# When the row sums leave PSUM, when they are used, and how the norm statistics are cut: three moves in a two-layer graph attention kernel

## The chip, the cores and the metric

The kernel runs on one core of a Trainium2 chip. The metric is the device time of one execution in microseconds (us). The core has a matrix engine (PE; its weight loads are listed apart as PEld), a vector engine (DVE), an activation engine (ACT), a general engine (POOL), and a queue engine (SP) that issues nearly all transfers. Each works through its own instructions in the order in which the program lists them; between engines there are semaphores.

## The reference, cut to what matters

There are 8 batch elements of 2048 nodes with 256 features, and one adjacency matrix for all. Layer 0 is masked attention with 4 heads of 64 features and a residual, with two layer norms behind it; layer 1 is a graph attention with two layer norms fewer:

```python
scores = clip(einsum(q, k) / 8, -10, 10);  scores = where(mask == 0, -10, scores)
attn = softmax(scores);  out = einsum(attn, v) @ Wo.T + bo + x
x = layernorm(x + layernorm(out) * gamma + beta)                      # end of layer 0
e = leaky_relu(s_i[:, None] + s_j[None, :]);  e = where(adj | eye, e, -inf)
x = layernorm(x + elu(softmax(e) @ Wh))                               # end of layer 1
```

A softmax in layer 0 runs over chunks of 256 keys, not over all 2048: every chunk has its own row sums, and the chunks' outputs are added after each is divided by its own sums.

## The kernel before, in words

**Layer 0.** An element has 4 blocks of 512 queries (`NIB`), and a block has 8 chunks of 256 keys (`NCH`). One chunk of one block is an iteration `J` (256 in all), and each has two halves of 128 keys. A half is called a beat here, after the counter `beat`; beats 0 to 511 are those of layer 0, 64 to an element. A beat has the scores of two pairs of heads (tile `sc`, L989, in the two buffers of a PSUM pool), their clipping and masking in place on DVE (L1004), and their exponentials on ACT (tile `e`, L1013). The products with v (tile `u`, L895, in two parts) and the row sums (tile `s`, L909: a product with ones) follow an iteration or more later. `s` and both `u` tiles come from one PSUM pool, `ps_m`, of two buffers. ACT copies them out: the sums to `ds` (L921), the products to `un` (L1055).

**From the sums to the division.** `inverses` (L917 to L948) copies the sums to `ds` and has SP send one row of each head to `dc` (L923), so that 128 partitions hold 16 values each. Then come, put on a list by beat (`at`): the reciprocal on DVE (L926), a store of it to DRAM (`rd`, L928), a load back that repeats each row for 32 partitions (`r`, L932), and `scaled`: the multiplication of `un` by `r` on DVE (L937 or L939) and, on POOL, its addition to `ctxT` (L940). What is on the list for a beat is emitted at the end of that beat.

**Layer 1 rides along.** When an element's layer 0 is done, its layer 1 runs inside the next element's beats: 64 steps of 128 keys by 512 queries. A step goes through ACT (`low` L723), DVE (`leaky` L727 and `edges` L732), ACT (`weights` L736), a POOL addition (`acc`, L747) and PE (`product`, L757, into the single PSUM buffer `us`). It is handed out at 1.5 steps per beat, so its 64 steps fill some 22 of the 32 iterations. Those are called open here, the others closed. In the code, `together` is true in an open iteration. There, half 0 has the sums of the iteration before the last (held back in the list `unsummed`, as POOL first has a transfer add the second half's exponentials to the first's, L1049) and both parts of `u`; half 1 has layer 1's products. In a closed iteration the sums and the first part of `u` are in half 0, the second part in half 1.

**Generators.** What stands behind a block is written as generators that advance one `yield` per beat. `fin` does layer 0's end of a block (projection `po`, two norms, transposes to `hT`), `fin1` that of layer 1 (tile `hx`, one norm, store to `out`, L620), `prelude` what layer 1 of an element needs first. `stats` (L310 to L322) has four pairs of bn_stats and bn_aggr on DVE (L315, L316), and one power on POOL (L321); `normalize` scales on ACT (L330). `short_pieces()` is true from beat 64 to beat 439. The tiles `x`, `y`, `hx` and `hr` have one buffer each.

What sets the order is the program text alone: nothing is reordered afterwards. The lines around the change:

Of the kernel before, what the change touches and what calls it, by code (L numbers as in the profile page):

```python
# [28 lines left out]
def tile_adj_attention__then__gat(  # L29
# [42 lines left out]
    NIB = N // IB  # L72
    TPB = IB // P
    NPAIR = H // 2
    NCH = N // CHUNK
# [234 lines left out]
    def stats(src, name):  # L310

        st = two.tile([P, TPB, 6], F32, tag="st", name=f"st_{name}")
        mv = two.tile([P, TPB, 2], F32, tag="mv", name=f"mv_{name}")
        for t in range(TPB):
            nc.vector.bn_stats(st[:, t, :], src[:, t, :])  # L315
            nc.vector.bn_aggr(mv[:, t, :], st[:, t, :])  # L316
            if t == TPB // 2 - 1 and beat < 2 * NIB * NCH:
                yield
        rstd = two.tile([P, TPB], F32, tag="rstd", name=f"rstd_{name}")
        nc.vector.tensor_scalar_add(rstd, mv[:, :, 1], EPS)  # L320
        nc.gpsimd.tensor_tensor(rstd, rstd, nhalf, ALU.pow)  # L321
        return mv, rstd  # L322
# [506 lines left out]
    def at(when, fn):  # L829
        agenda.setdefault(when, []).append(fn)  # L830
# [86 lines left out]
    def inverses(p, lag):  # L917


        ds = one.tile([P, IB], F32, tag="ds", name=f"ds{p['name']}")  # L920
        nc.scalar.copy(ds, p.pop("m"))  # L921
        p["dc"] = two.tile([P, IB // DH], F32, tag="dc", name=f"dc{p['name']}")
        nc.sync.dma_start(out=p["dc"], in_=ds.rearrange("(h m) (n w) -> h m n w", m=DH, n=DH)[:, 0, :, :])  # L923

        def inverse():
            nc.vector.reciprocal(p["dc"], p["dc"])  # L926
            p["rd"] = dram3.tile([H, IB], F32, tag="rd", name=f"rd{p['name']}")
            nc.sync.dma_start(out=p["rd"].rearrange("h (m w) -> (h m) w", m=DH), in_=p["dc"])  # L928

        def spread():  # L930
            p["r"] = two.tile([P, IB], F32, tag="r", name=f"r{p['name']}")
            nc.sync.dma_start(out=p["r"], in_=p["rd"].unsqueeze(1).to_broadcast([H, DH, IB]))  # L932

        def scaled():
            r2 = p["r"].unsqueeze(1).to_broadcast([P, 2, IB])
            if p["j"] == 0:
                nc.vector.tensor_mul(p["ctxT"], p["un"], r2)  # L937
            else:
                nc.vector.tensor_mul(p["un"], p["un"], r2)  # L939
                nc.gpsimd.tensor_add(p["ctxT"], p["ctxT"], p["un"])  # L940
            if p["j"] == NCH - 1:
                ctx_done[p["b"], p["ib"]] = beat
            if p["j"] == NCH - 3:
                fins.append(fin(p["b"], p["ib"], p["ctxT"]))

        at(beat + lag, inverse)
        at(beat + lag, spread)
        at(beat + 2 + 2 * lag, scaled)  # L948

    prev = None  # L950
    unsummed = []
# [1 line left out]
    for J in range(total + 1):  # L953
        b, ib, j = J // (NIB * NCH), J // NCH % NIB, J % NCH
        live = J < total
        if live and j == 0:
            ctxT = one.tile([P, 2, IB], F32, tag="ctx", name=f"ctxT{b}_{ib}")
        cur = {"b": b, "ib": ib, "j": j, "es": [], "ctxT": ctxT, "v": vs[min(b, B - 1)], "name": f"{b}_{ib}_{j}", "added": False}
        for half in range(2):
            c = 2 * j + half  # L960
            if live:

                if c % HT == 0:
                    if b == 0:
                        mk = blocks0[ib, c // HT]
                    else:
                        mk = mk0.pop((b, ib, c // HT))
                if c % HT == 1:
                    n = (b * NIB + ib) * 2 + c // HT + 1
                    nb, nib, nhf = n // (2 * NIB), n // 2 % NIB, n % 2  # L970
                    if 0 < nb < B:
                        mk0[nb, nib, nhf] = mask_block(0, nib, nhf, f"{nb}_{nib}_{nhf}")
            early = J < NIB * NCH
            rate = RATE if b < B - 1 else LAST_RATE
            if half == 0:
                together = prev is not None and live and l1_open()
            if not together:
                weights()
                waiting, flight["low"] = flight["low"], []
                take_lows(rate)  # L980
                new, flight["low"] = flight["low"], waiting
                leaky()
                flight["low"] = new
            scs = []
            if live:
                for hp in range(NPAIR):
                    sc = ps_s.tile([P, 2, IB], F32, tag="sc", name=f"sc{b}_{ib}_{c}_{hp}")
                    for h in range(2):
                        nc.tensor.matmul(  # L989
                            sc[:, h, :],  # L990
                            kTs[b][c // TPB][h * D : (h + 1) * D, hp, ts(c % TPB, P)],
                            qT[h * D : (h + 1) * D, hp, :],
                            start=True,
                            stop=True,
                        )
                    scs.append(sc)

            if half == 0:
                for p in unsummed:
                    sums(p)  # L1000
            if live:
                cap = mk[:, c % HT, :].unsqueeze(1).to_broadcast([P, 2, IB])
                for hp in range(NPAIR):
                    nc.vector.scalar_tensor_tensor(scs[hp], scs[hp], -CLIP, cap, ALU.max, ALU.min)  # L1004
                for hp in range(NPAIR):

                    e = one.tile(
                        [P, 2, IB],
                        F32,
                        tag=f"e{J % 2}_{(half + J // 2) % 2}_{hp}",  # L1010
                        name=f"e{b}_{ib}_{c}_{hp}",
                    )
                    nc.scalar.activation(e, scs[hp], AF.Exp)  # L1013
                    cur["es"].append(e)
                    if half == 0 and hp == 0:
                        for p in unsummed:
                            inverses(p, 0)
                        unsummed = []
            elif half == 0:
                for p in unsummed:  # L1020
                    inverses(p, 0)
                unsummed = []
            if not together:
                edges()
            elif half == 0:
                for s in flight["low"]:
                    s.leaky()
                    s.edges()
                flight["edged"] += flight["low"]
                flight["low"] = []  # L1030
            else:
                take_lows(2 * rate, 3.5)

            if prev is not None:
                if half == 0:
                    prev["un"] = three.tile([P, 2, IB], F32, tag="un", name=f"un{prev['name']}")
                    if not together:
                        sums(prev)
                        inverses(prev, 1 if early else 0)
                parts = (0, 1) if together and half == 0 else (half,) if not together else ()  # L1040
                ms = [ps_m.tile([P, IB], F32, tag="m", name=f"u{prev['name']}_{part}") for part in parts]
                for i in range(2):
                    for part, m in zip(parts, ms):
                        values(prev, part, m, i)
                    if together and half == 0 and i == 1:


                        for hp in range(NPAIR):
                            nc.gpsimd.dma_start(  # L1049
                                out=prev["es"][hp], in_=prev["es"][NPAIR + hp], accum_op=ALU.add  # L1050
                            )
                        prev["added"] = True
                        unsummed.append(prev)
                for part, m in zip(parts, ms):
                    nc.scalar.copy(prev["un"][:, part, :], m)  # L1055
            if together and half == 0:
                weights()

            end_beat(half == 1 or not together, half if together else None)
            if half == 1:  # L1060

                if live and j == NCH - 2 and J + 2 < total:
                    nb, nib = (b, ib + 1) if ib + 1 < NIB else (b + 1, 0)
                    xq = xT_tile(nb, nib, "q")
                if live and j == NCH - 1 and J + 1 < total:
                    qT = make_qT(nb, nib, xq)
            beat += 1
        prev = cur if live else None
# [55 lines left out]
```

## Time and profile before

| what | value |
|---|---|
| median of 3 runs | 4567.17 us (4559.63 to 4568.09) |
| the profiled execution's own time | 4558.66 us |
| its span, first to last instruction | 4556.9 us |
| busy: PE / DVE / ACT / POOL | 88% / 70% / 57% / 44% |
| granted clock of PE, mean | 0.957 |
| closed stretch of element 4, 2170 to 2320 us | PE 133.56 of 150.00 us busy, DVE 95.04, ACT 83.33 |
| open stretch of element 4, 2320 to 2710 us | PE 353.90 of 390.00 us busy, DVE 282.21, ACT 232.06 |
| after the last scores, 4269 to 4556 us | PE 191.73 of 287.00 us busy, DVE 222.25 |

The share of busy time is an average over stages with different limits, so each stage is read by itself. A wait in the profile is idle time of an engine just before an instruction, put down to what ended it. "PE u L895 <- ACT ds L921" reads: PE stood still ahead of a product of line 895 until ACT's copy of line 921 had been made. The two-buffer pool is why these are linked: the sums and the two parts of the product are three tiles.

### The profile page before, as it was taken

Reading aid. Unit: us, or ns where it says so; the run is one execution under the profiler, and the core shown is the slowest. Engines: PE = TensorE matmul, PEld = TensorE weight load, DVE = VectorE, ACT = ScalarE, POOL = GpSimd, SP = SyncE. Lnnn points to the kernel's source line nnn. Section 1 sums busy time; section 2 is a strip of 40 time slices with the busy share of each in tenths; the row PEclk is TensorE's granted clock in tenths of the full one; section 3 lists DMA queues with packets and bytes.
Section 4 is the critical chain, followed back from the end, with each engine's and each line's share of the span. In section 5 each row is a group of like instructions: output and inputs, shape, how many; then the busy total and the mean of one; then the engine's idle time right before and its main releaser. Section 6 shows DMA issues by size and latency. Waiting matters only on the chain. (4 is left out here: it accounts for less than half of the span.)

```text
span 4556.9 us, 59597 instructions
## 1 busy us (share of the span) xinstructions
PE 4004.2 (88%) x21845; PEld 1906.2 (42%) x21845; DVE 3188.2 (70%) x4530; ACT 2579.6 (57%) x3842; POOL 1989.5 (44%) x1203
## 2 busy tenths in 40 slices
PE   9889988899898888898899998899889899888767
PEld 3223334443344433444344543444334444344446
DVE  5886578755887557866588665876668756796777
ACT  5555555555566555655466555566555555565446
POOL 0232336553365434654346442555426545364520
PEclk9999999999999999999999999999999999999889
DMA  5554245543555435654356533655436554465521
GB/s 164 179 166 141 66 127 134 134 116 99 139 141 138 101 104 140 159 125 96 105 137 167 124 85 117 147 145 128 100 111 139 144 131 112 128 138 124 155 77 56
DMA packets 301125, 573.87 MB, mean 126 GB/s; under 512 B 90272, under 2 KB 125344, under 8 KB 299936
## 3 DMA queue, kind: packets, MB, share of 16 engines
q1 hardware_dynamic: 257344, 411.71, 30.3%
q0 software_dynamic: 43488, 158.35, 18.1%
q8 instruction: 171, 2.80, 0.3%
q14 instruction: 122, 1.00, 0.1%
HBM read 340.66 MB, written 68.88 MB: 90 GB/s over the span
## 5 line engine op out<-in xcount | busy, mean ns | idle before, releaser
L1013 ACT ACTIVATE e<-sc 128x1024 f32<-128x1024 f32 x1024 | 1045.6, 1026 | 1154.5 <-DVE sc L1004 1122.0
L1004 DVE SCALAR_TENSOR_TENSOR sc<-sc,mk 128x1024 f32<-128x1024 f32 x1024 | 1207.2, 1223 | 599.8 <-PE sc L989 498.7
L989 PE MATMUL sc<-qT,kT 64*128 64x512 f32 x4096 | 1079.1, 643 | 153.1 <-ACT e L1013 145.5
L895 PE MATMUL u<-e,v 128*32 128x512 f32 x8192 | 1011.9, 614 | 162.1 <-ACT ds L921 162.1
L757 PE MATMUL us<-wh,w 128*128 128x256 f32 x3584 | 854.7, 394 | 101.1 <-ACT w L736 53.3
L940 POOL TENSOR_TENSOR ctxT<-ctxT,un 128x1024 f32<-128x1024 f32 x224 | 569.0, 2540 | 696.6 <-DVE un L939 615.7
L757 PEld LDWEIGHTS us<-wh,w 128*128 128x128 f32 x3584 | 685.1, 195 | 322.3 <-ACT w L736 149.6
L747 POOL TENSOR_TENSOR acc<-acc,w 128x512 f32<-128x512 f32 x392 | 605.2, 1544 | 155.5 <-ACT w L736 136.0
L989 PEld LDWEIGHTS sc<-qT,kT 64*128 64x128 f32 x4096 | 354.8, 191 | 739.6 <-issue 356.8
L1049 POOL DMA_DIRECT2D e<-e x302 | 269.5, 1034 | 882.5 <-PE u L895 869.5
L895 PEld LDWEIGHTS u<-e,v 128*32 128x32 f32 x8192 | 244.3, 112 | 865.0 <-issue 519.6
L1055 ACT COPY un<-u 128x512 f32<-128x512 f32 x512 | 299.4, 586 | 284.8 <-PE u L895 270.2
L732 DVE TENSOR_TENSOR w<-w,mk 128x512 f32<-128x512 f32 x512 | 381.9, 746 | 40.9 <-DMA mk<-mask 23.9
L727 DVE SCALAR_TENSOR_TENSOR w<-ab,sj,w 128x512 f32<-128x512 f32 x512 | 406.6, 795 | 3.9 <-ACT w L723 3.9
L442 DVE CUSTOM_DVE_ANT_0 fb<-sj_row,fb 128x1024 bf16<-128x1024 f32 x240 | 377.0, 1594 | 18.7 <-DMA fb<-far 18.7
L909 PE MATMUL s<-e,ones 128*32 128x512 f32 x2888 | 372.3, 616 | 0.2 <-ACT hT L388 0.2
L939 DVE TENSOR_TENSOR un<-un,r 128x1024 f32<-128x1024 f32 x224 | 289.7, 1294 | 85.1 <-DMA r<-rd 76.8
L723 ACT ACTIVATE w<-ab,sj 128x512 f32<-128x512 f32 x512 | 336.2, 712 | 3.8 <-DMA ab<-ab_d 3.8
L736 ACT ACTIVATE w<-w 128x512 f32<-128x512 f32 x512 | 294.1, 625 | 73.8 <-DVE w L732 73.0
L321 POOL TENSOR_TENSOR rstd_a<-rstd_a,nhalf 128x4 f32<-128x4 f32 x32 | 45.6, 1424 | 333.4 <-DVE rstd_a L320 333.4
L909 PEld LDWEIGHTS s<-e,ones 128*32 128x32 f32 x2888 | 70.2, 111 | 279.4 <-issue 244.9
L361 PE MATMUL po<-WT_o,ctxT 128*128 128x256 f32 x512 | 136.9, 426 | 54.2 <-POOL ctxT L940 38.3
(113 smaller groups left out, 3202.4 us busy)
## 6 DMA issues: line engine op xcount, KB each, us to landing
e<-e POOLq DMA_DIRECT2D x302, 512.0 KB, 6.4
r<-rd SPq DMA_DIRECT2D x256, 256.0 KB
mk<-mask SPq DMA_DIRECT2D x120, 512.0 KB
fb<-far SPq DMA_DIRECT2D x240, 256.0 KB
xT_k<-in_xT_dram SPq DMA_DIRECT2D x32, 512.0 KB
raw<-in_adjT_dram SPq DMA_DIRECT2D x32, 512.0 KB
rawf<-in_adj_dram SPq DMA_DIRECT2D x32, 512.0 KB
x<-in_x_dram SPq DMA_DIRECT2D x32, 512.0 KB
```

The costliest lines, as they stand in the source:

```text
L442: nc.vector.tensor_tensor_reduce(out=fb, in0=row, in1=fb, scale=1.0, scalar=2 * FAR * 0.999, op0=ALU.add, op1=ALU.max, accum_out=dst,)
L723: nc.scalar.activation(self.w, k["ab"][:, 1, :], AF.Identity, bias=k["sj"][:, 1, c : c + 1])
L727: nc.vector.scalar_tensor_tensor(self.w, k["ab"][:, 0, :], k["sj"][:, 0, c : c + 1], self.w, ALU.add, ALU.max)
L732: nc.vector.tensor_tensor(self.w, self.w, self.k["mks"][self.c // HT][:, self.c % HT, :], ALU.min)
L747: nc.gpsimd.tensor_add(k["acc"], k["acc"], self.w)
L757: nc.tensor.matmul(k["us"][:, t, :], self.w[:, ts(t, P)], k["wh"][c // TPB][:, c % TPB, 0:F], start=(first and t % 2 == 0), stop=last, ski ...
L895: nc.tensor.matmul(m[h * DH : (h + 1) * DH, :], p["v"][pc // TPB][:, pc % TPB, f0 : f0 + DH], p["es"][2 * i + h // 2][:, h % 2, :], start= ...
L909: nc.tensor.matmul(m[h * DH : (h + 1) * DH, :], ones[:, 0:DH], p["es"][2 * i + h // 2][:, h % 2, :], start=(i == 0), stop=(i == tiles - 1),)
L940: nc.gpsimd.tensor_add(p["ctxT"], p["ctxT"], p["un"])
L989: nc.tensor.matmul(sc[:, h, :], kTs[b][c // TPB][h * D : (h + 1) * D, hp, ts(c % TPB, P)], qT[h * D : (h + 1) * D, hp, :], start=True, sto ...
L1004: nc.vector.scalar_tensor_tensor(scs[hp], scs[hp], -CLIP, cap, ALU.max, ALU.min)
L1013: nc.scalar.activation(e, scs[hp], AF.Exp)
```

## The change

1. The copy of the sums. In an open iteration, and in the first closed one after an open stretch, `inverses` for the held-back sums is called directly after their matmuls are emitted. Before, its copy (and the transfer to `dc`) stood between the two exponentials of half 0; now it stands ahead of both.
2. The product with the reciprocals. Where the sums were not added beforehand (`p["added"]` false) and layer 0 still runs, `scaled` is emitted 3 beats after the sums and no longer 2. In element 0 (`lag` of 1) it was 4 and is 4; for the added ones it was 2 and is 2. So it moves in the closed iterations of elements 1 to 7.
3. The statistics. `stats` yields after its second pair in all elements up to beat 439, and not in element 0 alone. Each `fin` so takes two beats more and each `fin1` one more.

```diff
@@ stats
-            if t == TPB // 2 - 1 and beat < 2 * NIB * NCH:
+            if t == TPB // 2 - 1 and (beat < 2 * NIB * NCH or short_pieces()):
                 yield
@@ inverses
         at(beat + lag, inverse)
         at(beat + lag, spread)
-        at(beat + 2 + 2 * lag, scaled)
+        at(beat + (2 if p["added"] or beat >= 2 * total else 3 + lag), scaled)
@@ main loop
             if half == 0:
                 for p in unsummed:
                     sums(p)
+                    inverses(p, 0)
+                unsummed = []
             if live:
                 cap = mk[:, c % HT, :].unsqueeze(1).to_broadcast([P, 2, IB])
                 for hp in range(NPAIR):
...
                     nc.scalar.activation(e, scs[hp], AF.Exp)
                     cur["es"].append(e)
-                    if half == 0 and hp == 0:
-                        for p in unsummed:
-                            inverses(p, 0)
-                        unsummed = []
-            elif half == 0:
-                for p in unsummed:
-                    inverses(p, 0)
-                unsummed = []
```

No instruction is added or taken away on any engine: the counts are those of before. In the order of the instructions, the later `fin` puts all of a layer 1 (its preparation, its 64 steps, its ends) 2 to 4 beats later against layer 0 in elements 0 to 5, and 0 to 2 beats later in element 6. As many iterations are open as before, 151.

## The prediction

> **What bounds the kernel now.** I read the page first. Its span is 4556.9 us, the execution's own time 4558.66, the median of the runs 4567.17: sums are made against 4559, and 8 us are added at the end to stand beside the runs.
>
> ```profile
> PE 4004.2 (88%) x21845; PEld 1906.2 (42%) x21845; DVE 3188.2 (70%) x4530; ACT 2579.6 (57%) x3842; POOL 1989.5 (44%) x1203
> ```
>
> PE is the fullest engine, and no stage has another: 90% in the open stretches, 83 to 90% in the closed ones. It idles for some 540 us. Sorting its idle time by iteration gives 275.6 us in the 151 open iterations (mean 18.40 us long), 133.2 in the 73 closed ones of elements 1 to 7 (mean 14.47), 42.3 in element 0, 81.3 behind the last scores. What ends it is in the list of waits:
>
> ```profile
> PE u L895 <- ACT ds L921: 162.1, 145, 6.1
> DVE dc L926 <- DMA dc<-ds: 159.5, 65, 8.9
> ...
> PE sc L989 <- ACT e L1013: 145.5, 58, 6.3
> ...
> DVE un L939 <- DMA r<-rd: 76.8, 30, 5.8
> ```
>
> The columns are us in total, times, longest. The first line is PE's largest wait, and it is the one that the first edit touches: 145.2 us of it lie in open iterations and 15.4 in the first closed ones. The timeline of a half 0 shows where it comes from (start, duration, engine and line; in brackets the idle time before). Two halves of element 4; the first has DVE late, the second has not:
>
> ```profile
> 2013.34 1.07 PE L909 MATMUL s<-e,ones 128*32 128x512 f32 x8
> ...
> 2015.80 1.02 ACT L1013 ACTIVATE e<-sc 128x1024 f32<-128x1024 f32 x1 [3.69 <-DVE sc L1004]
> 2016.72 0.58 ACT L921 COPY ds<-s 128x512 f32<-128x512 f32 x1
> ...
> 2017.36 2.78 PE L895 MATMUL u<-e,v 128*32 128x512 f32 x24 [2.10 <-ACT ds L921]
> ...
> 2029.88 1.02 ACT L1013 ACTIVATE e<-sc 128x1024 f32<-128x1024 f32 x1
> ...
> 2030.80 0.58 ACT L921 COPY ds<-s 128x512 f32<-128x512 f32 x1
> ...
> 2031.43 2.78 PE L895 MATMUL u<-e,v 128*32 128x512 f32 x24 [0.22 <-ACT ds L921]
> ```
>
> The sums are ready at 2014.4. Their copy sits behind an exponential that waits for DVE, ACT idles 3.69 us with the copy at hand, and the second part of `u` can't start, since `s` holds its buffer. Of the open iterations, 60 have over 0.5 us of this (126.9 us in all, most 2.0 to 3.2), 91 the small one (18.3 us). The closed stretch is another story:
>
> ```profile
> 2190.09 1.22 DVE L939 TENSOR_TENSOR un<-un,r 128x1024 f32<-128x1024 f32 x1 [5.54 <-DMA r<-rd]
> 2191.44 0.25 DVE L926 RECIPROCAL dc<-dc 128x16 f32<-128x16 f32 x1
> 2191.61 2.33 DVE L1004 SCALAR_TENSOR_TENSOR sc<-sc,mk 128x1024 f32<-128x1024 f32 x2
> ```
>
> ```profile
> 2193.93 3.34 PE L989 MATMUL sc<-qT,kT 64*128 64x512 f32 x8 [3.77 <-ACT e L1013]
> ```
>
> DVE waits 5.54 us for `r`, the clipping stands behind it, the exponential behind that, and PE loses 3.77 us.
>
> **What the Trainium skill says.** "PSUM — Partial Sum Buffer", section "Engine vs sequencer instructions": the queues of ScalarE and VectorE are strictly first in, first out, and matmuls start in program order. The trace agrees: ACT idles 3.69 us ahead of the exponential with the copy's input long made. "DMA: Bandwidth & Descriptors", section "Anatomy of one DMA — SWDGE (gpsimd) path": about 2.0 us of a transfer are fixed, mostly the receipt of the last write. Here, where nothing is in the way, `dc` lands 1.9 us after its issue. "Perfetto Trace Analysis", section "Tensor Engine Instruction (MATMUL, LD_WEIGHTS)": the ends of matmuls are estimated, so I trust PE's gaps to some 0.1 us.
>
> **The copy ahead of both exponentials.** New order on ACT: copy, exponential, exponential. In a normal half PE has scores 1.99, sums 1.07 and the first quarter of `u` 1.04 us. The sums end 3.0 us after the scores' start, the copy runs from 3.2 to 3.8, and the second part of `u` is due at 4.0: no wait. Where DVE is late the copy no longer knows of it. Working this through every open iteration by its own times leaves about 4 of the 145.2 us. The price: the first exponential moves from 2.5 to 3.7 us after the scores' start, in some 100 iterations by 1.1 us on the mean, the second by 0.7. Its cover is `u`: the next scores stand behind four quarters of it, start at 6.8, and need the first exponential's buffer (free at 4.7) and at 7.8 the second's (5.6). So nothing is paid up to a lateness of DVE of some 2 to 3 us. Without that cover it would be 100 x 1.1 = 110 us.
>
> What is late next is DVE itself. It is busy 13.4 of 18.4 us in the mean, but not evenly: where the wait is 3.2 us (the 20th and the 28th iteration of each element), DVE idles only 1.2 to 1.8 in the whole iteration, so PE would run into the clipping one or two beats on. Taking in each open iteration the smaller of PE's wait and DVE's idle time gives 104 us. With the 15.4 of the first closed ones, and something lost to the in-order coupling of the other engines, I take 90. The ends are 40 (PE meets DVE each time) and 150.
>
> **The product a beat later.** `scaled` is one DVE product of 1.22 us and one POOL addition of 2.4; no transfer moves with it. In the closed half 0 the order is now clipping, reciprocal, clipping of half 1; before, the product with its wait for `r` stood ahead of the reciprocal. The 27 waits of closed iterations are 75.3 us. What they are worth is bounded by `dc`, which lands about 1.95 us after its issue and which the reciprocal still waits for (84.1 us in closed ones). Taking the product out of every closed half 0, and letting the next clipping wait for the latest of DVE, `dc` and its scores, brings that clipping forward by 43 us in sum: 3 to 4.4 in the second closed iteration of an element, and little elsewhere. PE idles behind nearly all of it (41 us). Against it stands the product's new place, ahead of half 0's clipping: 1.22 us where DVE has no gap there, some 3 iterations in each of 7 elements, 26 us at most; half of these had no wait for `dc` to lose, where the move is even. 41 less 13, and a third for what other queues eat: 20. Ends: -10 and 40. The projection `po` of a block that ends closed is a beat later too, which goes with the next edit.
>
> **The statistics in two pieces.** No instruction more. Four pairs take 2.35 us of DVE in one beat (0.43 + 0.18, the rest overlapping at 0.52 a pair), and now 1.2 and 1.2. In the open iterations with 3.2 us of wait they stand between `po`'s additions and the next clipping, so DVE is 1.2 us less late there: that supports the first edit's sum more than it adds. I add 5. What the extra beats cost: `hx` has one buffer. Its store (L620) now starts a beat later, and the next block's copy into `hx` (L784) waits for its landing on ACT, ahead of the next exponentials. From store to copy there are 20 us from first to second block, 34 from second to third and 11.5 from third to fourth; a beat is 7 to 9. The last handover keeps 3 to 4 us, and in four stores looked at the last packet ends 2.5 to 7.4 us after the issue. So 2 us are lost in each of 6 elements, 12 in all (0 to 30). The tail behind layer 0 has one step of layer 1 more on PE, 4 x 0.39, 2 us. Together -9; ends -40 and +25, since every load and store of the ends meets other neighbours on SP.
>
> **Sum.** 90 + 20 - 9 = 101 us less: 4559 - 101 = 4458 for the execution, 4466 beside the runs.
>
> **Rivals.** *DVE takes over.* PE runs ahead until its scores wait for exponentials, and the wait for the copy comes back as "PE sc <- ACT e". For it: DVE's idle time of 0.3 us in the 22nd, 25th and 30th iteration of an element. Against: 5.0 us idle in the mean open iteration, and iterations of 6 to 8 us idle between the tight ones. Then the first edit gives 40 and the others 5 together: 4567 - 45 = 4522. *The moves do nothing for each other and only the copy's small part counts*, because the late halves are late through a chain over POOL and ACT that sets the pace whatever PE does: 18 us, and the rest is eaten by the store: 4555 to 4567, the same or nearly. Against it: layer 1's ends span many beats, and PE is 90% full between them. *Slower: the store of `hx` comes too late.* Its place is the copy L784 of the second to fourth blocks of six elements, 18 handovers, and it bears if the store shares the rings with the 512 KB loads of `x`, `xT` and `hT`. A transfer of 8 KB so crowded took 12 us from issue to landing (2477.07 to 2489.10, DVE waiting 7.2). It decides from 101 / 18 = 5.6 us a handover; at 8 us it is 144 against 101, or 4610. Against it: only one of three handovers is near at all. So it would need the first edit to fall short too.
>
> **How the numbers follow.** As summed: 0.55, own range 4410 to 4510. DVE takes over: 0.24. The same or nearly: 0.07, of which most is within 0.2% (9 us, about what a measurement of this kernel can tell from no change). Slower: 0.14. Faster is then 0.55 + 0.24 + 0.02 = 0.81, same 0.05, slower 0.14. The low end takes the favourable ends of the first two edits, 4567 - 150 - 15 = 4402. The high end reaches over no change into the slower case, to 4575, which leaves out a tenth.
>
> **What will show it.** Right: the wait of `u` for `ds` falls from 162 to under 20 us; open iterations fall by 0.5 us or more in the mean; PE's busy time stays at 4004 and its share rises to 90%; "DVE un <- DMA r" falls under 40 us with `dc`'s wait up a little. If DVE takes over, "PE sc <- ACT e" grows from 145.5 by about what `u` loses. If the store is the bound, a wait of ACT's L784 for the transfer of `hx` appears, which today has none. The prediction is wrong above all if the late halves of DVE pass on whole to the next scores.

## The result, and the profile after

The kernel with the three edits takes 4546.4 us (median of 10 runs) against 4567.6 of the kernel before on the same chip. The ratio is 0.9957, with a 95% interval of 0.9946 to 0.9967: 0.43% faster, some 20 us, where 101 were forecast. The profiled execution has a span of 4544.3 us and took 4546.4 itself, 12 us less than the one before.

The page of the changed kernel, first its engines, then the groups that answer to those that matter here (busy us, then mean ns of one):

```profile
PE 3998.4 (88%) x21845; PEld 1897.5 (42%) x21845; DVE 3357.3 (74%) x4530; ACT 2586.8 (57%) x3842; POOL 2019.7 (44%) x1203
...
L1006 DVE SCALAR_TENSOR_TENSOR sc<-sc,mk 128x1024 f32<-128x1024 f32 x1024 | 1205.1, 1220 | 560.7 <-PE sc L989 529.2
...
L727 DVE SCALAR_TENSOR_TENSOR w<-ab,sj,w 128x512 f32<-128x512 f32 x512 | 449.3, 878 | 4.4 <-ACT w L723 4.4
L732 DVE TENSOR_TENSOR w<-w,mk 128x512 f32<-128x512 f32 x512 | 431.6, 844 | 22.5 <-DMA mk<-mask 5.5
...
L442 DVE CUSTOM_DVE_ANT_0 fb<-sj_row,fb 128x1024 bf16<-128x1024 f32 x240 | 402.0, 1694 | 22.5 <-DMA fb<-far 22.4
```

DVE is busy 169 us longer, 3357.3 against 3188.2, with the very same 4530 instructions. The clipping (L1006, L1004 before) has kept its 1.22 us. The leaky inputs (L727) went from a mean of 795 ns to 878, the edges (L732) from 746 to 844, `fb` (L442) from 1594 to 1694.

The list of waits of the changed kernel:

```profile
DVE dc L926 <- DMA dc<-ds: 173.4, 52, 9.8
PE sc L989 <- ACT e L1015: 172.3, 95, 7.2
...
PE us L757 <- ACT hx L784: 87.4, 14, 9.9
PE us L757 <- ACT w L736: 69.8, 53, 17.4
...
PE pq L255 <- ACT un L1049: 31.1, 12, 5.5
...
PE u L895 <- ACT ds L921: 26.0, 29, 2.5
...
DVE dc L926 <- issue: 25.9, 5, 7.8
...
DVE dc L926 <- DMA hTl<-hT_d: 25.2, 3, 8.5
...
PE pq L255 <- DMA xT_q<-in_xT_dram: 17.0, 9, 3.8
```

Both targeted waits are gone: PE's for `ds` fell from 162.1 to 26.0 us, DVE's for `r` from 76.8 to 4.0. But of PE's 136 us, 124 stand in other rows: scores behind exponentials 27 more, `us` behind `hx` 40 more and behind `w` 16 more, `pq` 41 more (2.1 + 4.7 before). And in the closed iterations the reciprocal's waits, all three rows together, went from 84 to 202 us.

One iteration shows how DVE is late without a gap of its own. First DVE in the 22nd iteration of element 4 (start, duration, instruction), then POOL beside it:

```profile
2391.09 2.47 DVE L442 CUSTOM_DVE_ANT_0 fb<-sj_row,fb 128x1024 bf16<-128x1024 f32 x1
...
2393.49 3.39 DVE L442 CUSTOM_DVE_ANT_0 fb<-sj_row,fb 128x1024 bf16<-128x1024 f32 x1
...
2396.82 2.35 DVE L1006 SCALAR_TENSOR_TENSOR sc<-sc,mk 128x1024 f32<-128x1024 f32 x2
2399.08 0.73 DVE L727 SCALAR_TENSOR_TENSOR w<-ab,sj,w 128x512 f32<-128x512 f32 x1
...
2401.85 1.77 DVE L727 SCALAR_TENSOR_TENSOR w<-ab,sj,w 128x512 f32<-128x512 f32 x1
2403.65 1.64 DVE L732 TENSOR_TENSOR w<-w,mk 128x512 f32<-128x512 f32 x1
...
2407.57 2.34 DVE L1006 SCALAR_TENSOR_TENSOR sc<-sc,mk 128x1024 f32<-128x1024 f32 x2
2409.81 1.22 DVE L442 CUSTOM_DVE_ANT_0 fb<-sj_row,fb 128x1024 bf16<-128x1024 f32 x1
```

```profile
2390.11 2.37 POOL L940 TENSOR_TENSOR ctxT<-ctxT,un 128x1024 f32<-128x1024 f32 x1
2392.43 3.37 POOL L374 TENSOR_TENSOR y<-y,gamma_bc 128x1024 f32<-128x1024 f32 x1
2395.88 3.23 POOL L375 TENSOR_TENSOR y<-y,x 128x1024 f32<-128x1024 f32 x1
...
2401.80 2.95 POOL L747 TENSOR_TENSOR acc<-acc,w 128x512 f32<-128x512 f32 x2 [0.97 <-ACT w L736]
2407.57 2.34 POOL L940 TENSOR_TENSOR ctxT<-ctxT,un 128x1024 f32<-128x1024 f32 x1 [2.82 <-DVE un L939]
```

`fb` takes 1.22 us at 2409.81, where POOL is through 0.1 us later, and 2.47 and 3.39 us beside POOL. Both times it ends 1.08 us after POOL's instruction does (2393.56 after 2392.48, 2396.88 after 2395.80): it stood still until POOL was done. It goes the other way too: POOL's L374 and L375, which began while an `fb` was under way, take 3.37 and 3.23 us, while the shortest of their lines take 2.35 and 2.36. The third leaky input and its edges take 1.77 and 1.64 us beside `acc`, against 0.73 and 0.69 alone. The Trainium skill says just this: "SBUF — State Buffer", section "Who interferes with whom", states that an instruction of VectorE with two inputs in SBUF contends with one of GpSimd that reads SBUF, and that the later of the two is blocked until the first is done. The operations that stretch here have two or more inputs in SBUF; the clipping, whose scores are in PSUM, takes 1198 to 1233 ns in all 1024 cases, `acc` beside it or not. One case could be chance, so I went through all 1488 instructions of lines 442, 727, 732 and 939 in the changed kernel: 996 have no POOL operation beside them (its issues of transfers not counted), and none of these is more than 10 ns over the median of its line. Each that is over 150 ns longer has one beside it.

The lateness comes out at PE by way of ACT:

```profile
2408.81 2.15 ACT L1015 ACTIVATE e<-sc 128x1024 f32<-128x1024 f32 x2 [2.85 <-DVE sc L1006]
2410.86 1.93 ACT L723 ACTIVATE w<-ab,sj 128x512 f32<-128x512 f32 x3
2412.70 0.99 ACT L784 COPY hx<-us 128x1024 f32<-128x1024 f32 x1
```

```profile
2413.74 3.78 PE L757 MATMUL us<-wh,w 128*128 128x256 f32 x8 [8.25 <-ACT hx L784]
```

The copy of `us` into `hx` waits its turn behind late exponentials and three leaky inputs, and PE stands for 8.25 us.

For the experiments I use two sums per element, means over elements 2 to 6: the 6th to 16th iteration, where layer 1 is closed (give or take one at each end), and the other 21. A move of layer 1 by a beat or two blurs them less than it does the count of open and closed iterations. Before they are 161.2 and 388.6 us, after 165.7 and 382.7. So the middle of the kernel has gained 1.4 us per element; the rest of the profile's 12 us is the first element with layer 1 beside it (538.2 to 517.0), less what element 0, the last element and the tail lost. What made that one element faster was not taken apart; each edit alone brings it down as well (509.7 to 529.4).

### The profile page after: what moved, and what is told of

Read it like the earlier page. It is cut to its first block, busy times and chain, and to the rows that moved or that the text cites. A ratio compares the mean times of both kernels' runs of the same rounds, so it can differ in the third digit from the quotient of the medians.

```text
span 4544.3 us, 59493 instructions
## 1 busy us (share of the span) xinstructions
PE 3998.4 (88%) x21845; PEld 1897.5 (42%) x21845; DVE 3357.3 (74%) x4530; ACT 2586.8 (57%) x3842; POOL 2019.7 (44%) x1203
## 5 line engine op out<-in xcount | busy, mean ns | idle before, releaser
L1006 DVE SCALAR_TENSOR_TENSOR sc<-sc,mk 128x1024 f32<-128x1024 f32 x1024 | 1205.1, 1220 | 560.7 <-PE sc L989 529.2
L1015 ACT ACTIVATE e<-sc 128x1024 f32<-128x1024 f32 x1024 | 1033.5, 1024 | 849.2 <-DVE sc L1006 810.3
L989 PE MATMUL sc<-qT,kT 64*128 64x512 f32 x4096 | 1090.6, 645 | 173.0 <-ACT e L1015 172.3
L895 PE MATMUL u<-e,v 128*32 128x512 f32 x8192 | 965.9, 596 | 26.1 <-ACT ds L921 26.0
L747 POOL TENSOR_TENSOR acc<-acc,w 128x512 f32<-128x512 f32 x392 | 612.1, 1561 | 195.6 <-ACT w L736 178.4
L727 DVE SCALAR_TENSOR_TENSOR w<-ab,sj,w 128x512 f32<-128x512 f32 x512 | 449.3, 878 | 4.4 <-ACT w L723 4.4
L732 DVE TENSOR_TENSOR w<-w,mk 128x512 f32<-128x512 f32 x512 | 431.6, 844 | 22.5 <-DMA mk<-mask 5.5
L736 ACT ACTIVATE w<-w 128x512 f32<-128x512 f32 x512 | 306.7, 629 | 209.3 <-DVE w L732 208.0
L442 DVE CUSTOM_DVE_ANT_0 fb<-sj_row,fb 128x1024 bf16<-128x1024 f32 x240 | 402.0, 1694 | 22.5 <-DMA fb<-far 22.4
L921 ACT COPY ds<-s 128x512 f32<-128x512 f32 x256 | 148.8, 581 | 383.6 <-issue 246.3
L723 ACT ACTIVATE w<-ab,sj 128x512 f32<-128x512 f32 x512 | 336.1, 711 | 1.4 <-DMA ab<-ab_d 1.4
L939 DVE TENSOR_TENSOR un<-un,r 128x1024 f32<-128x1024 f32 x224 | 308.8, 1379 | 4.0 <-DMA r<-rd 4.0
L926 DVE RECIPROCAL dc<-dc 128x16 f32<-128x16 f32 x256 | 61.9, 244 | 224.7 <-DMA dc<-ds 173.4
```

The source lines that it names most:

```text
L442: nc.vector.tensor_tensor_reduce(out=fb, in0=row, in1=fb, scale=1.0, scalar=2 * FAR * 0.999, op0=ALU.add, op1=ALU.max, accum_out=dst,)
L723: nc.scalar.activation(self.w, k["ab"][:, 1, :], AF.Identity, bias=k["sj"][:, 1, c : c + 1])
L727: nc.vector.scalar_tensor_tensor(self.w, k["ab"][:, 0, :], k["sj"][:, 0, c : c + 1], self.w, ALU.add, ALU.max)
L732: nc.vector.tensor_tensor(self.w, self.w, self.k["mks"][self.c // HT][:, self.c % HT, :], ALU.min)
L747: nc.gpsimd.tensor_add(k["acc"], k["acc"], self.w)
L895: nc.tensor.matmul(m[h * DH : (h + 1) * DH, :], p["v"][pc // TPB][:, pc % TPB, f0 : f0 + DH], p["es"][2 * i + h // 2][:, h % 2, :], start= ...
```

## The experiments

**One edit alone.** `copy` has the first edit only, `scaled` the second, `stats` the third.

```diff
 copy:   after sums(p)      +  inverses(p, 0)      (and removed between the exponentials)
 scaled:                    -  at(beat + 2 + 2 * lag, scaled)
                            +  at(beat + (2 if p["added"] or beat >= 2 * total else 3 + lag), scaled)
 stats:                     -  if t == TPB // 2 - 1 and beat < 2 * NIB * NCH:
                            +  if t == TPB // 2 - 1 and (beat < 2 * NIB * NCH or short_pieces()):
```

> First edit alone (the copy of the sums ahead of both exponentials). Theory 1, DVE takes over: the wait of u for ds falls from 162 us to under 30, but DVE, late and slowed where POOL works beside it, hands its lateness to the scores and to layer 1's handovers; DVE's busy time rises by 80 to 170 us over 3188 and the kernel is 10 to 40 us faster. Theory 2, the other two edits eat the gain: this one alone is 80 to 110 us faster, DVE's busy time about as before.

> Second edit alone (the product with the reciprocals a beat later in closed iterations). Prediction: 10 to 30 us faster, closed iterations at 14.2 us in the mean and less, DVE's wait for r under 10 us, its wait for dc up from 159.5. Theory 2: dc's wait takes all of r's 75 us and the product's new place costs more, 0 to 40 us slower.

> Third edit alone (statistics in two pieces everywhere, layer 1 two beats later). Prediction: within 15 us of before. As the waits of DVE for POOL's y (75 us) lie in the beat that the second piece moves, theory 1 lets it gain 5 to 30 us even without the copy. Theory 2: 20 to 40 us slower through other neighbours on the queues.

Measured: the copy 4537.5 us, ratio 0.9934 (0.9912 to 0.9956), 30 us; the product 4563.9, 0.9992 (0.9979 to 1.0004), nothing; the statistics 4566.9, 0.9993 (0.9980 to 1.0006), nothing. With the copy alone PE's wait for `ds` is 14.8 us, DVE is busy 3288.2, a hundred more than before, and the scores wait 168.6 for exponentials against 145.5. With the product alone DVE's two waits trade places:

```profile
DVE dc L926 <- DMA dc<-ds: 260.8, 67, 9.1
...
DVE un L939 <- DMA r<-rd: 3.5, 6, 1.5
```

73 us less for `r`, 101 more for `dc`. The copy's gain and DVE's rise are those of its first theory; the product's forecast, 10 to 30 us, failed. The three alone make 30 us; together they make 20. So they are not independent.

**Pairs.** Each of the three leaves one edit of the changed kernel out: `scaled_stats` the copy, `copy_scaled` the statistics, `copy_stats` the product.

```diff
 (against the changed kernel)
 scaled_stats:  inverses(p, 0) back between the two exponentials of half 0
 copy_stats:    -  at(beat + (2 if p["added"] or beat >= 2 * total else 3 + lag), scaled)
                +  at(beat + 2 + 2 * lag, scaled)
 copy_scaled:   -  if t == TPB // 2 - 1 and (beat < 2 * NIB * NCH or short_pieces()):
                +  if t == TPB // 2 - 1 and beat < 2 * NIB * NCH:
```

> The changed kernel with the copy put back between the exponentials. Theory 1: the copy is worth little, this one lies within 25 us of the changed kernel (4546). Theory 2: the copy is worth 80 to 110 us, so this one is at 4620 or more.

> First and third edit, the product with the reciprocals left where it was. The copy alone ran at 0.9934, the statistics alone at 0.9993, the product and the statistics together at 1.0047. If the loss is of that pair, this one keeps the copy's gain, 0.990 to 0.994. If the statistics' later layer 1 costs whatever stands beside it, 0.996 or more.

> First and second edit, the statistics left whole. If the loss is of the pair of product and statistics, this one keeps the copy's gain, 0.990 to 0.994. If the product's new place costs beside the copy (DVE is then the tighter engine and pays its 1.22 us in every closed iteration), 0.996 or more.

Measured: second and third 4588.0, 1.0047 (1.0030 to 1.0064), slower than before; first and third 4514.6, 0.9894 (0.9875 to 0.9913), faster than all three; first and second 4530.9, 0.9927 (0.9908 to 0.9946). The first of these lies between its two theories; the other two keep the copy's gain, so the loss is of the pair. The copy is worth 30 us alone and 42 to 52 beside the statistics. The statistics are worth nothing alone and 23 beside the copy: with it the other 21 iterations fall from 387.0 to 380.0 us per element and the 6th to 16th rise from 158.8 to 163.1. Of these, 4.1 and 2.0 us are PE's own busy time, which in part moves with layer 1 from the one to the other; the rest is idle time. The product is worth nothing alone or with the copy, and costs 21 us beside the statistics and 32 beside both. These are differences of medians; the ratios put each within some 7 us of them.

**POOL's additions left out.** The 420 additions of layer 1's row sums (L745, L747) are not made, and 28 constant fills stand in for them; layer 1 is then divided by a constant. In `before_noacc` nothing else is changed; `copy_noacc` has the first edit too, `after_noacc` all three.

```diff
-                nc.gpsimd.tensor_add(k["acc"], k.pop("w0"), self.w)
-            else:
-                nc.gpsimd.tensor_add(k["acc"], k["acc"], self.w)
+                nc.gpsimd.memset(k["acc"], 1.0)
```

> The kernel before, without the 420 additions on POOL that make layer 1's row sums (a constant stands for them, so layer 1 is divided by a constant). It is the base for the same cut in the kernel with the first edit. DVE's busy time falls by 40 to 80 us from 3188 if POOL's additions slow it; PE's wait of u for ds stays above 120 us; the time is 0 to 30 us less.

> The first edit with the same 420 additions left out. Theory 1 (DVE is slowed where POOL works beside it, and that eats the copy's gain): DVE's products L727 and L732 stay at 0.75 and 0.70 us, DVE's busy time rises by under 60 us against the base with the same cut, where it rose by some 120 with the additions, and the copy is worth 60 us or more here. Rival (DVE's order alone hands the lateness on, at whatever speed): the copy is worth 20 to 40 us here as well.

> All three edits, with POOL's 420 additions of layer 1's row sums left out (the sums are constants, so layer 1's divisor is not the reference's). Beside the kernel before with the same cut (4522.7 us) and the first edit with it (4439.7 us). If the second and third edits are worth what the prediction gave them once DVE keeps its durations (+20 and -9, together +11): 4420 to 4435 us. If the later product costs through dc whatever POOL does: 4445 to 4475 us, with dc's wait in closed iterations still above 150 us.

Measured: 4522.7, 4439.7 and 4435.5 us, ratios 0.9904 (0.9882 to 0.9927), 0.9722 (0.9699 to 0.9745) and 0.9715 (0.9694 to 0.9736). Without the additions the copy is worth 83 us, not 30. The engines of the first edit alone, then without the additions the kernel before and the first edit:

```profile
PE 4012.6 (88%) x21845; PEld 1910.7 (42%) x21845; DVE 3288.2 (72%) x4530; ACT 2592.8 (57%) x3842; POOL 1990.1 (44%) x1203
```

```profile
PE 3993.6 (88%) x21845; PEld 1898.9 (42%) x21845; DVE 3179.4 (70%) x4530; ACT 2576.6 (57%) x3842; POOL 1338.2 (30%) x811
PE 3960.5 (89%) x21845; PEld 1891.2 (43%) x21845; DVE 3174.7 (72%) x4530; ACT 2585.1 (58%) x3842; POOL 1339.0 (30%) x811
```

With the additions the copy makes DVE busy 100 us longer; without them it makes it 5 us shorter (3179.4 to 3174.7). I also summed, for lines 727, 732, 442 and 939, what each instruction took over the median of its line: 159 us before, 293 with the copy, 297 after; without the additions 210, and 211 with the copy. So the copy as such doesn't stretch DVE: it moves DVE's work to times at which POOL adds. Four expectations failed, though. In the kernel before, leaving the additions out took 9 us off DVE's busy time and not 40 to 80, as other POOL operations then run beside DVE; it took 45 us off the kernel and not up to 30; PE's wait for `ds` fell to 109.3 us and didn't stay above 120; and with the copy too L727 and L732 stay at means of 0.89 and 0.83 us and don't come down to 0.75 and 0.70.

Nor is all of the 83 us waiting. In the profiles, 94 us apart, PE's idle time falls by 61 us and its busy time, for the same 21845 matmuls, by 33 (granted clock 0.956 and 0.963). With the additions the copy takes 28 us off PE's idle time and puts 8 on its busy time (clock 0.957 and 0.955). Set against what the copy takes from PE's wait for `ds`, 61 of 100 us stay gained without the additions (109.3 to 9.5), with them 28 of 147 (162.1 to 14.8). Why the granted clock differs from kernel to kernel was not tested.

One reservation: leaving the additions out also frees 650 us of POOL, so this pair alone doesn't separate the blocking from a shorter queue on POOL. The waits speak for the blocking as what the copy meets: with the copy, the idle time that POOL ends falls from 118.7 to 90.0 us on DVE and rises only from 38.3 to 42.5 on PE, while DVE's operations get 134 us longer. In the kernel before the queue does count, as without the additions these waits are 18.7 and 10.8 us.

With all three edits and no additions the other 21 iterations take 369.2 us per element, 22.0 less than before without additions, but the 6th to 16th take 163.3, which is 4.9 more. The loss in the closed stretch is another matter than POOL's additions: DVE's waits ahead of the reciprocal are still 204 us there. The run stands at the edge of its first theory's range and has this sign of the second.

**The reciprocal a beat later.** `after_lag` has all three edits, and in every closed iteration the reciprocal and its store one beat later and the product four beats after the sums. `before_lag` is the kernel before with the same one word changed (its product then comes two beats later), `copy_lag` that with the first edit.

```diff
-                        inverses(prev, 1 if early else 0)
+                        inverses(prev, 1 if live else 0)
```

> All three edits, and in every closed iteration the reciprocal, too, goes a beat later (and the product four beats after the sums, one more than in after), so that DVE no longer comes to the reciprocal before the 16 values of dc have landed. In after DVE waits 202 us for dc in closed iterations. Theory A, that wait is what the second edit costs beside the third: dc's wait in closed iterations falls under 40 us, closed iterations fall from 14.98 to at most 14.7 us in the mean, and the ratio to before is at most 0.990, at or under the kernel without the second edit (0.9894). Theory B, the cost is what the product and its addition on POOL meet at their later place: dc's wait falls all the same, but the ratio stays at 0.994 to 0.999.

> The kernel before, and in every closed iteration the reciprocal a beat later and the product two beats later, nothing else: copy, statistics and the rest where they were. Before, DVE waits 84 us for dc and 75 us for r in closed iterations (mean 14.47 us). Theory A, in the closed stretches the transfer of the sums sets the pace by itself, and the second edit took r's wait away and left dc's: both waits fall under 20 us each, closed iterations fall to 13.8 to 14.0 us, ratio 0.989 to 0.994 (some 30 to 45 us). Theory B, dc's wait costs only where the third edit has moved the ends of the blocks: closed iterations stay at 14.3 to 14.6 and the ratio at 0.997 to 1.003.

> The first edit, and in every closed iteration the reciprocal a beat and the product two beats later; no statistics in two pieces. Beside the first edit alone (0.9934) and all three with the later reciprocal (0.9762). Theory A of the kernel before with the same move: closed iterations at 13.8 to 14.0 us against 14.28, and a ratio of 0.985 to 0.989; the statistics are then worth 40 to 50 us in the open iterations, as they are from the first edit alone (18.33) to the first and third (17.97). Theory B: closed iterations at 14.2 or more, ratio 0.991 to 0.996.

Measured: all edits with it 4452.0 us, 0.9762 (0.9738 to 0.9786), some 90 us below the changed kernel (in the profiles 99, of which 31 are PE's busy time, at a granted clock of 0.965 against 0.958); the kernel before with it 4558.7, 0.9981 (0.9970 to 0.9992); the copy with it 4537.5, 0.9937 (0.9922 to 0.9953). In the first, closed iterations fell from a mean of 14.98 to 13.90 us, and the row of `dc` is:

```profile
DVE dc L926 <- DMA dc<-ds: 45.4, 25, 6.9
```

So the wait for `dc` is what the changed kernel pays in its closed stretch. But the kernel before fitted neither theory, nor did the copy: closed iterations fell by more than forecast, 14.47 to 13.41, as did both waits (18 and 1 us left in them), and the time didn't follow, since open iterations rose from 18.41 to 18.95 (with the copy 14.28 to 13.27, and 18.33 to 18.84). Of the 81 us of that rise 36 are PE's busy time, in an execution whose granted clock is 0.948 against 0.957; 45 are idle time. A new row in its list of waits, where 4.7 us stood before, and then its timeline ahead of the first open iteration of element 4:

```profile
PE pq L255 <- DMA xT_q<-in_xT_dram: 45.2, 9, 7.2
```

```profile
2296.88 0.38 SPq L928 DMA_DIRECT2D rd<-dc  x1
...
2299.93 1.82 POOL L1049 DMA_DIRECT2D e<-e  x2 [6.83 <-PE u L895]
2300.32 0.54 SPq L932 DMA_DIRECT2D r<-rd  x1
2300.94 0.43 SPq L119 DMA_DIRECT2D xT_q<-in_xT_dram  x1
...
2313.31 2.04 PE L255 MATMUL pq<-xT_q,WT_q 128*128 128x512 f32 x2 [6.63 <-DMA xT_q<-in_xT_dram]
```

The moved `r` holds SP until `rd` is stored; the 512 KB load of the next queries is issued behind it, a microsecond after POOL's two transfers of 512 KB, and the product finds it 12.4 us later. That iteration takes 24.0 us, before 16.0 (with the copy 24.1 against 15.7). With all three edits, where it is a closed one, it takes 17.8 us, and the later reciprocal pays.

**That load a beat earlier.** `before_lag_xq` adds one move.

```diff
-            if half == 1:
+            if half == 0:
                 if live and j == NCH - 2 and J + 2 < total:
                     nb, nib = (b, ib + 1) if ib + 1 < NIB else (b + 1, 0)
                     xq = xT_tile(nb, nib, "q")
```

> The kernel before with the later reciprocal in closed iterations (0.9981), and the load of xT_q one beat earlier, before the transfers of the later reciprocal are handed to SP. With the later reciprocal alone closed iterations fell from 14.47 to 13.41 us (78 us in all), but the open ones rose by 81 us, 40 us of it in a new wait of PE for xT_q in the first open iteration of a block of elements 2 to 6, where the load was issued behind r and beside POOL's two transfers of 512 KB, and took 12 us. Theory A, the gain is given back by that load: the wait of PE for xT_q falls from 45 us to under 10, the iteration at 24.0 us to 16 to 18, and the ratio to 0.987 to 0.992. Theory B, the gain is eaten by whatever comes later in the open iterations: the wait goes, but the time comes back in the next ones, ratio 0.996 to 1.000.

Measured: 4503.0 us, 0.9854 (0.9834 to 0.9874), some 56 us better than without this move, and 66 us below before: more than theory A had. The wait for `xT_q` is gone, the iteration is back at 15.9 us (about 40 us over five elements), and 8 us come from element 0, where the same load was late. This shows that the load took most of what the later reciprocal gave. The earlier load was not run by itself; in the kernel before, PE waits for it only 4.7 us. It doesn't account for all: the other 21 iterations stay at 396.8 us per element against 388.6 before, 5 us of it in the 19th. About half of these 8.2 us, 4.4, is PE's busy time, at a granted clock of 0.955 in these iterations against 0.967. What is behind the rest stays open; beside the copy and the statistics it isn't seen (379.6 with the later reciprocal, 382.7 without).

**ACT's queue, and the fastest version.** `ct_lows` is the first and third edit with the leaky inputs of half 1 (three L723 of 0.65 us, which stand ahead of the copy of `hx` above) issued behind the half's end. `lag_lows` adds this to `after_lag`, and `lag_lows_xq` the earlier load as well.

```diff
-            else:
-                take_lows(2 * rate, 3.5)
...
             end_beat(half == 1 or not together, half if together else None)
+            if together and half == 1:
+                take_lows(2 * rate, 3.5)
```

> The first and the third edit, and layer 1's leaky inputs of half 1 (three or four ACT instructions L723 of 0.7 us) are issued behind the end of the half rather than ahead of it, so that they no longer stand ahead of the copy of hx L784 on ACT. Theory A, PE's waits for that copy are ACT's queue: 'PE us L757 <- ACT hx' falls from 87 us to 50 or less, and the ratio is 0.985 to 0.988. Theory B, DVE's lateness sets when the copy can run: the wait for hx or its neighbours take the same time, ratio 0.988 to 0.992, the same as without the move.

> All three edits, the later reciprocal in closed iterations, and layer 1's leaky inputs of half 1 issued behind the end of the half. The later reciprocal alone gave 0.9762, the later inputs alone 0.9883 beside 0.9894. If the two add: 0.973 to 0.976, with PE's wait for hx under 65 us (87.5 without the second move) and dc's wait in closed iterations under 40. If DVE's lateness takes up what ACT gives: 0.976 to 0.979.

> All three edits, the later reciprocal, the later inputs of layer 1 (0.9746 with these), and the load of xT_q one beat earlier. PE's wait for xT_q was 27.6 us with the later reciprocal. If it goes and nothing comes in its place: 0.968 to 0.972. If the load now meets other transfers: 0.973 to 0.978.

Measured: 4513.2 (0.9883, 0.9863 to 0.9903), 4443.6 (0.9746, 0.9728 to 0.9764) and 4417.6 us (0.9673, 0.9656 to 0.9690). In the first, PE's wait for `hx` falls from 81.0 to 62.1 us, less than forecast, and the ratio isn't told from the 0.9894 without the move, while PE waits 7 us more for exponentials. This is what the theory of DVE's lateness expected; it doesn't show that DVE sets the pace. The second isn't told from `after_lag` either. The earlier load is worth some 30 us more, and the last kernel is the fastest of all, 3.3% faster than before and some 130 us below the changed kernel. Its engines:

```profile
PE 3958.6 (90%) x21845; PEld 1887.2 (43%) x21845; DVE 3342.9 (76%) x4530; ACT 2589.5 (59%) x3842; POOL 2012.9 (46%) x1203
```

PE has the 90% that the prediction looked for, though with 40 us less busy time than in the changed kernel (granted clock 0.969 against 0.958). DVE is nearly as stretched as there: 287 us over the medians.

## Why the prediction was wrong

The side was right, the size a fifth of the forecast; and more of the profile's gain lies in one element (21 us) than in the next five together (7), which the forecast didn't expect. Each term of the sum was off:

- **"What is late next is DVE itself … I take 90."** This step failed first. It took DVE's idle time (5.0 us in the mean open iteration) at DVE's durations of before. Measured alone: 30. As PE no longer waits, DVE's work falls beside POOL's additions and stands still behind them, 134 us more over the medians; idle time that was to hide the lateness is spent. Where POOL makes no additions, and the copy doesn't lengthen DVE's work, the same edit gives 83, 61 of them in PE's waits. The prediction took 90 of the 160 us of wait for `ds` as gain; there 61 of 100 us stayed gained, with the additions 28 of 147. As far as this pair shows, then, the working was near right for a DVE whose work the edit doesn't lengthen, and the step failed on the lengthening. The rival "DVE takes over" was nearest, by a mechanism that it didn't name. The trace of before already showed it: `fb` had a mean of 1594 ns against 1.22 us where it ran alone, and the page of the skill named above has the rule. I read the mean of a row as the price of an operation. A reading beside it was off too: of the 3.69 us that ACT idled "with the copy at hand", the sums were ready (2014.4) for the last 1.4 only. The sum used PE's own 2.10 us, so it doesn't change.
- **"Taking the product out of every closed half 0 … brings that clipping forward by 43 us … 20."** Measured nothing alone, and 21 to 32 us of loss beside the statistics. `r`'s wait ran while `dc` was under way; without it DVE came to the reciprocal that much sooner and waited there for `dc`, up to 9.8 us at a time. The step said itself that `dc` bounds the gain, and then took 41 us from it. The edit that does what this one meant is the later reciprocal; in the kernel before it needs the load of `xT_q` moved to pay, beside all three edits it pays as it stands.
- **"The projection `po` of a block that ends closed is a beat later too, which goes with the next edit"** and the statistics' "together -9". The sign of the sum was wrong in both directions: beside the copy the halved statistics take 7.0 us per element off the other 21 iterations and put 4.3 us on the 6th to 16th (in idle time 2.9 and 2.3). Net 23 us gained. I had 5 for the first and little for the second. That the first comes of a DVE that is less late, and the second of the ends that moved, is argued and not shown.
- **The store of `hx`, 12 us, and the rival "slower".** The sign came, small: from the store's issue to the next copy 3.5 to 5.8 us are left at the nearest handovers, eleven of them, but ACT's L784 waits for the store only four times, 4.8 us in all and at most 2.2. PE's wait for that copy grew by 40 us; in the case shown, late exponentials and the inputs ahead of it on ACT held it.
- **The signs to look for.** `u` for `ds` at 26.0 (under 20 forecast; 14.8 with the copy alone), `r` at 4.0 (under 40). Open iterations fell by 0.38 us, not 0.5, and closed ones rose from 14.47 to 14.98. The 16th is now counted as closed in place of the 6th; over the 6th to 16th together the rise is 0.41 us each. PE's share stayed at 88%. The sign for "DVE takes over" was too narrow: "PE sc <- ACT e" took back 27 of 136 us, while the rest came back at `us` and `pq`, where the waits name ACT and a load.

That the three terms are coupled is the larger lesson: 30, 0 and 0 us alone, 53 for the best pair, 20 for all.

## What to carry to other kernels

An engine's idle time is not room for more overlap if its operations are held up by a neighbour that is also half idle: before counting on it, compare the mean of each row with its shortest case, and see what ran beside the long ones. When a wait is taken from in front of an instruction, look at what that instruction itself waits for, and when a transfer is moved, at the loads queued behind it on the same engine: here 78 us gained in one stretch were lost in the next, about half of it to a load issued late. And part a gain into PE's idle and busy time before explaining it by waits.

## What was not expected of the hardware

A POOL operation held up the `fb` of DVE that began behind it until it had ended itself: `fb` went from 1.22 to 3.39 us. In the changed kernel this lengthened DVE's work by 297 us over four lines, 159 already before. That isn't kernel time: with the later reciprocal the stretch is the same (296) and the kernel some 90 us faster. A clipping with the scores in PSUM and only the mask in SBUF never took more than 1.233 us in 1024 cases. The same 21845 matmuls kept PE busy for 4024 us in the profile with the lowest granted clock, 0.948, and for 3959 in the one with the highest, 0.969. And two transfers of 512 KB on POOL's queue ahead of a third on SP's went with 12.4 us until the third could be used; that the two caused it was not tested alone.
